# A gated attention and expert layer: which queues carry the gates' spread rows, which engine normalizes rows, and how a logarithm is corrected

## The chip, the cores and the metric

The kernel runs on one core of one Trainium2 chip, in float32. The core has five engines that run at the same time and meet through semaphores: TensorE (PE; its weight loads are listed apart as PEld), VectorE (DVE), ScalarE (ACT), GpSimd (POOL) and SyncE (SP), which only issues DMAs. Each engine takes its instructions strictly in the order that the compiled program gives it. The metric is the time of one execution on the device, in microseconds (us).

## What is computed

The reference takes x and ctx, both of shape (8, 512, 1024), so 4096 tokens of 1024 numbers. Cut to what matters:

```
n  = layernorm(x)                      # rows: (x - mean) / sqrt(var + eps)
ig = [n, ctx, ctx] @ Wi + bi           # 16 heads: input gates
fg = [n, ctx, ctx] @ Wf + bf           # forget gates
log_f = log_sigmoid(fg);  cum = cumsum of log_f along the sequence
log_D[s, t] = cum[s] - cum[t] + ig[t]  for t <= s, else -inf
D  = exp(log_D - max over t)
C  = (n_h ctx_h^T / 8) * D             # each head has 64 columns
h  = C / (max(|row sum of C|, exp(-max)) + 1e-6) @ ctx_h
x  = x + tanh(g_xattn) * layernorm of h over each head * ln_scale
y  = layernorm(x)
x  = x + tanh(g_ffn) * (shared(y) + the two best of 16 experts(y), weighted)
```

`shared` and each expert are silu(y Wg) * (y Wu) Wd.

## The kernel before, in words

**Tiles and stages.** The 4096 tokens are 32 tiles of 128 rows (four to a sequence, NT = 32, NS = 4). The first stage runs the attention over the tiles in a loop (L882 to L941) and fills TensorE's free places with units of the shared network for the first 20 tiles (`shared_units`, L225; a chunk is 16 matmuls or 16 of a projection down, and `fill` runs the next ones that the loop's shares allow). Then the tokens are gathered expert by expert (from L1301 on); that second stage is not touched by the change.

**One turn of the loop, for tile i.** It starts with the transposes of tile i+1's normalized rows (`prep_queries`, from `q.xn` to qT). `prep_weights` turns the spread gates `q.d` into weights: 16 exponents on ScalarE, each with a column of `q.cols` as bias (L603). `scores(i, 0)` multiplies qT and kT into two PSUM banks (`psc`), and VectorE multiplies the banks into d (L619). `prep_keys` transposes the context rows of tile i+1 (`q.kv` to kT). `head_norm(i - 1)` finishes the attention of the tile before on VectorE (L699 to L701). After a filler, `gate_products` and `prep_gates` make the gates of tile i+1, then `finish_rows(i - 1)` normalizes the finished rows to y, `values` multiplies weights and context (`pav`), `turn_rows(i - 1)` transposes y, `head_scale` and `grow` end the tile: `grow` adds the products `pst` to the running `state`, whose adds on VectorE (L672) free the banks that the next `psc` takes. `prep_columns(i + 1)` comes before the last filler.

**The gates (`prep_gates`, L485).** One matmul (`pg`) sums the partial products. log_sigmoid(f) is min(f, 0) - log(1 + z), with z = exp(-|f|). The logarithm is taken of the rounded u = 1 + z and corrected by the factor z / (u - 1), with a case for u = 1. Then come a running sum (`cum`), a running maximum (`m`), nm = -m, and e = exp(m of the tile before - m). The rows nm and e hold 16 heads x 128 tokens; their values are needed by all partitions. So each is written to DRAM (`nm_d`, `e_d`) and read back spread over 128 partitions: `q.d` (1 MB, one DMA) and `q.eb` (two DMAs of 256 KB, 512 pieces each). Tile 0 needs neither, and the first tile of each sequence has no e. All of these DMAs, like all loads and stores, are issued by SP, in one order.

**prep_columns (L553).** It transposes the gate rows to columns (`pc`, `cols`), masks `q.d` on GpSimd (L561), takes `decay` out of eb and multiplies eb by qT on VectorE (L567, L568), and scales the context for `grow` (`wv`).

**Normalizing a row tile.** `row_stats` (L124) takes mean and variance on VectorE. `inverse_deviation` (L115) adds eps and raises to -0.5 on GpSimd (`ve`, `rstd`). `normed` (L450) subtracts and multiplies on VectorE:

```
def normed(row, mean, rstd):
    o = wk.tile([P, D], F32, tag="row", name="row", bufs=2)
    normed.last = nc.vector.tensor_scalar(o, row, mean, rstd, ALU.subtract, ALU.mult).ins
    return o
```

It is used twice for each tile: for x two tiles ahead (`prep_norm`) and for y (`finish_rows`).

**What sets the order.** The loop is only the order of writing. A list scheduler with estimated durations places each instruction on its engine's queue; `tc.issue_after` and `pinned` hold an instruction behind a given other one. `behind` is the last matmul of the last filler unit. Buffers of a tile pool are reused in rotation (`bufs`); a load waits until the users of its buffer are done. Context rows `kv` have two buffers, x rows three.

Of the kernel before, what the change touches and what calls it, by code (L numbers as in the profile page):

```python
# [46 lines left out]
def flamingo_layer(  # L47
# [20 lines left out]
    nc = tc.nc  # L68
# [55 lines left out]
    def row_stats(pool, row):  # L124

        st = pool.tile([P, 2, 6], F32, tag="bst", name="bst")
        for k in range(2):
            nc.vector.bn_stats(st[:, k, :], row[:, k * 512 : (k + 1) * 512])
# [157 lines left out]
    def pinned(stack, ins):  # L286

        if ins:
            stack.enter_context(tc.issue_after(ins[0]))
# [20 lines left out]
    with ExitStack() as actx:  # L310
# [15 lines left out]

        def load_kv(i: int):
            q, b, c = toks[i], i // NS, i % NS
            q.kv = wk.tile([P, D], F32, tag="kv", name="kv")
            nc.sync.dma_start(q.kv, ctx_in[b, c * P : (c + 1) * P, :])  # L330

        load_x(0)
# [6 lines left out]
        nc.scalar.dma_start(w3[:, :, NH:], wf.rearrange("(c p) h -> p c h", p=P))  # L339
        bias_i = ac.tile([NH, 1], F32, name="bias_i")  # L340
        bias_f = ac.tile([NH, 1], F32, name="bias_f")
        nc.scalar.dma_start(bias_i, bi.unsqueeze(1))
        nc.scalar.dma_start(bias_f, bf.unsqueeze(1))
        ones_p = ac.tile([P, P], F32, name="ones_p")
        nc.gpsimd.memset(ones_p, 1.0)
        ones = ones_p[:NH, :]
# [33 lines left out]


        lnsc = ac.tile([P, D], F32, name="lnsc")
        nc.scalar.dma_start(lnsc, ln_scale.unsqueeze(0).to_broadcast([P, D]))


        sums = ac.tile([P, 48], F32, name="sums")
# [18 lines left out]
        nc.scalar.dma_start(acc_d[T : T + P, :], zeros[:, :D])  # L405
# [13 lines left out]
        def prep_router():  # L419
            nc.vector.tensor_scalar(lnsc, lnsc, tgx, None, ALU.mult)  # L420
            rw = wk.tile([NE, D], F32, tag="u", name="rw", bufs=1)
            nc.scalar.dma_start(rw, router_w)
# [24 lines left out]
            nc.scalar.copy(parts, pp)  # L447
            return parts

        def normed(row, mean, rstd):  # L450
            o = wk.tile([P, D], F32, tag="row", name="row", bufs=2)
            normed.last = nc.vector.tensor_scalar(o, row, mean, rstd, ALU.subtract, ALU.mult).ins
            return o

        def prep_norm(i: int):
            q = toks[i]
            mv = row_stats(sm, q.x)
            rstd = inverse_deviation(sm, mv[:, 1:2], LN_EPS, [P, 1])
            q.xn = normed(q.x, mv[:, 0:1], rstd)

        def prep_values(i: int):
            q = toks[i]
# [22 lines left out]
        def prep_gates(i: int, after=()):  # L485
            q, last, first = toks[i], i % NS == NS - 1, i % NS == 0
            pg = ps.tile([48, P], F32, tag="tr", name="pg")
            with ExitStack() as order:
                pinned(order, after)
                nc.tensor.matmul(pg, lhsT=sums, rhs=q.parts, start=True, stop=True)  # L490

            def row(name, bufs=2):
                return gt.tile([NH, P], F32, tag=name, name=name, bufs=bufs)

            f = row("f", 1)
            a, en, w = (rows3[i % 2][32 * k : 32 * k + NH, :] for k in range(3))
            nc.scalar.copy(f, pg[32:48, :])
            nc.vector.tensor_scalar(a, pg[0:NH, :], bias_i, None, ALU.add)
            nc.vector.tensor_scalar(f, f, bias_f, None, ALU.add)


            z, u, lnu, eq = (row(n, 1) for n in ("z", "u", "lnu", "eq"))
# [20 lines left out]
            nc.vector.tensor_tensor_scan(  # L523
                q.m, a, a, LOWEST if first else before.m[:, P - 1 : P], ALU.max, ALU.max
            )
            nm = row("nm", 1)
            nc.vector.tensor_scalar(nm, q.m, -1.0, None, ALU.mult)

            q.d = wk.tile([P, NH, P], F32, tag="d", name="d")
            if i > 0:  # L530
                nc.sync.dma_start(nm_d[i], nm)
                nc.sync.dma_start(q.d, nm_d[i].unsqueeze(0).to_broadcast([P, NH, P]))
            else:
                q.nm = nm
            if not first:

                e = row("e", 1)
                nc.scalar.activation(e, q.m, AF.Exp, bias=before.m[:, P - 1 : P], scale=-1.0)
                nc.sync.dma_start(e_d[i], e)
                q.eb = wk.tile([P, NC, P], F32, tag="eb", name="eb")  # L540
                for hh in range(2):
                    nc.sync.dma_start(
                        q.eb[hh * DH : (hh + 1) * DH, :, :],
                        e_d[i].rearrange("(c a) s -> a c s", a=2)[hh]
                        .unsqueeze(0).to_broadcast([DH, NC, P]),
                    )

            nc.vector.tensor_add(en, q.cum, q.m)
            nc.scalar.activation(en, en, AF.Exp, scale=-1.0)
            if not last:  # L550
                nc.scalar.activation(w, a, AF.Exp, bias=nm[:, P - 1 : P])

        def prep_columns(i: int):  # L553
            q, last, first = toks[i], i % NS == NS - 1, i % NS == 0
            pc = ps.tile([P, 5, NH], F32, tag="tr", name="pc")
            nc.tensor.transpose(pc.rearrange("p k h -> p (k h)"), rows3[i % 2], ident[:80, :80])
# [8 lines left out]
            if not first:  # L565
                q.decay = sm.tile([P, NC], F32, tag="decay", name="decay", bufs=2)
                nc.vector.tensor_copy(q.decay, q.eb[:, :, P - 1])  # L567
                nc.vector.scalar_tensor_tensor(  # L568
                    q.eb, q.eb, DH**-0.5, q.qT, ALU.mult, ALU.mult
                )  # L570
# [132 lines left out]
        def finish_rows(i: int):  # L703
            q = toks[i]
            nc.sync.dma_start(x1_d[i] if i < NT - 4 * HELD else acc_d[i * P : (i + 1) * P, :], q.x)
            mv = row_stats(sm, q.x)
            rstd = inverse_deviation(sm, mv[:, 1:2], LN_EPS, [P, 1])
            q.y = normed(q.x, mv[:, 0:1], rstd)
            nc.sync.dma_start(y_d[i * P : (i + 1) * P, :], q.y)

        def turn_rows(i: int):
# [126 lines left out]
        prep_norm(0)  # L838
        prep_queries(0)
        prep_keys(0)  # L840
        with tc.issue_after(normed.last):
# [5 lines left out]
        with tc.issue_after(normed.last):  # L847
            prep_norm(1)
        with tc.issue_after(normed.last):
            prep_router()  # L850
        prep_weights(0, 0)
        prep_weights(0, 1)
# [29 lines left out]
        for i in range(1, NT):  # L882
# [651 lines left out]
```

## Time and profile before

| what | value |
|---|---|
| median of 3 runs | 3168.99 us (3162.78 to 3174.18) |
| the profiled execution | 3176.98 us, span 3174.8 us |
| VectorE, ScalarE, GpSimd busy | 56%, 27%, 41% of the span |
| L452 row (VectorE) | 64 times, 52.3 us, mean 817 ns |
| L510 reciprocal (VectorE) | 32 times, 30.0 us, mean 936 ns |
| L561 mask on d (GpSimd) | 31 times, 63.8 us, mean 2057 ns |
| DMA d, from issue to landing | median 5.6 us |
| DMA eb, from issue to landing | median 6.9 us |
| DMA nm_d and e_d, from issue to landing | median 2.0 us each |
| DMA kv, from issue to landing | median 6.0 us |

The page shows one execution. Its first lines give the busy time of each engine; then follow the span in 40 equal slices (busy tenths, and under PEclk the granted clock of TensorE in tenths). "A <- B" behind a wait means that A stood still until B was done. A queue with a q (SPq) is the part of an engine that issues DMAs. In the timeline a row starts with its start and its length in us; what stands in brackets is the idle time ahead of it and what ended that.

### The profile page before, as it was taken

How to read it: one execution, taken by the hardware profiler on the slowest of the kernel's cores; microseconds unless marked ns; L12 is line 12 of the kernel's file. 1: busy time of each engine (PE TensorE's matmuls, PEld its weight loads, DVE VectorE, ACT ScalarE, POOL GpSimd, SP SyncE). 2: the span in 40 equal slices, each digit the busy share in tenths (PEclk: the TensorE clock that was granted, in tenths of full speed). 3: DMA queues.
4: the chain of work that ended last, by engine and by line, in shares of the span. 5: the costliest groups of instructions: out<-in, count | busy, mean ns of one | idle time of the engine just before them, and what ended most of it. 6: DMA issues, size and time to landing. Idle time of an engine off the chain costs nothing.

```text
span 3174.8 us, 42502 instructions
## 1 busy us (share of the span) xinstructions
PE 3055.4 (96%) x16193; PEld 2290.9 (72%) x16193; DVE 1792.3 (56%) x3597; ACT 859.1 (27%) x1823; POOL 1295.8 (41%) x1019
## 2 busy tenths in 40 slices
PE   6999989999999999998999999999999999999999
PEld 5778777776877768676666677777777777767776
DVE  5655656666767766653444444444544554555554
ACT  3544443544444534411111111111111111100000
POOL 2212231323232222316555555555665545444442
PEclk7989999999999999999999999999999999999999
DMA  6776565665666566545554444554555544644330
GB/s 196 207 222 184 180 168 174 178 202 164 201 177 195 181 177 188 164 131 209 136 136 119 127 134 135 134 139 134 141 141 142 149 113 133 211 161 158 113 126 27
DMA packets 371103, 500.59 MB, mean 158 GB/s; under 512 B 24304, under 2 KB 263072, under 8 KB 366768
## 3 DMA queue, kind: packets, MB, share of 16 engines
q1 hardware_dynamic: 342560, 425.00, 42.8%
q0 software_dynamic: 24576, 71.52, 10.7%
q8 instruction: 130, 2.13, 0.3%
q10 hardware_dynamic: 3760, 1.31, 0.2%
q14 instruction: 77, 0.63, 0.1%
HBM read 394.57 MB, written 113.69 MB: 160 GB/s over the span
## 4 chain that ended last, share of the span: by engine, by line
PE 50%; DVE 4%; issue 0%; DMA 0%; POOL 0%; DVEq 0%
PE pq L1330 47%; PE ptx L1248 2%; DVE hsum L1398 1%; PE pq L1437 1%; DVE hT L1352 1%; DVE hsum L1399 1%; DVE up L1351 0%; DVE tsum L1279 0%; DMA gat<-y_d,tok_i 0%; DVE tsum L1276 0%; DVE tsum L1277 0%; DVE yo L1409 0%; DVE xT L1251 0%; DVE u L1416 0%; DVE u L1415 0%
## 5 line engine op out<-in xcount | busy, mean ns | idle before, releaser
L1330 PE MATMUL pq<-xT,w 128*128 128x256 f32 (+12 forms) x2112 | 496.9, 385 | 8.6 <-DVEq L1311 8.6
L1330 PEld LDWEIGHTS pq<-xT,w 128*128 128x128 f32 x2112 | 401.3, 190 | 83.5 <-issue 11.0
L1330 PE MATMUL pq<-tsum,wsum 128*128 128x256 f32 (+12 forms) x1408 | 339.4, 384 | 0.0
L252 PE MATMUL pgu<-sh_yT,swg 128*128 128x256 f32 (+1 forms) x1280 | 299.7, 384 | 0.6 <-DMA swg<-L_ffn_shared_gate_w_dram 0.6
L1330 PEld LDWEIGHTS pq<-tsum,wsum 128*128 128x128 f32 x1408 | 264.0, 190 | 40.0
L269 PE MATMUL pso<-sh_down,sh_hT 128*128 128x512 f32 x640 | 286.6, 599 | 0.9 <-DVE sh_hT L258 0.9
L252 PE MATMUL pgu<-sh_yT,swu 128*128 128x256 f32 (+1 forms) x1280 | 276.2, 369 | 0.9 <-DMA swu<-n_L_ffn_shared_up_w_dram 0.9
L252 PEld LDWEIGHTS pgu<-sh_yT,swg 128*128 128x128 f32 x1280 | 233.7, 197 | 33.0 <-issue 3.6
L252 PEld LDWEIGHTS pgu<-sh_yT,swu 128*128 128x128 f32 x1280 | 233.7, 190 | 31.0 <-DMA swu<-n_L_ffn_shared_up_w_dram 1.3
L118 POOL TENSOR_SCALAR ve<-bmv 128x1 f32<-128x1 f32 x64 | 15.6, 243 | 576.3 <-DVE bmv L130 574.2
L1354 DVE TENSOR_TENSOR hT<-pq,u 128x256 f32<-128x256 f32 (+12 forms) x176 | 75.7, 430 | 299.1 <-PE pq L1330 294.1
L1295 POOL TENSOR_TENSOR wsum<-w 128x512 f32<-128x512 f32 x88 | 113.5, 1289 | 277.7 <-PE pq L1330 275.1
L269 PEld LDWEIGHTS pso<-sh_down,sh_hT 128*128 128x128 f32 x640 | 119.1, 192 | 135.2 <-issue 132.2
L1351 DVE TENSOR_TENSOR up<-pq,u 128x256 f32<-128x256 f32 (+12 forms) x176 | 75.6, 429 | 211.8 <-PE pq L1330 210.4
L1053 POOL DMA_INDIRECT acc_d<-yo,row_i x64 | 102.1, 1595 | 189.8 <-ACT yo L1427 81.5
L1330 PE MATMUL pq<-wd,hT 128*128 128x512 f32 x352 | 169.9, 598 | 7.1 <-DVE hT L1352 5.4
L1330 PE MATMUL pq<-tsum,w 128*128 128x256 f32 (+12 forms) x704 | 169.6, 384 | 0.0
L1330 PE MATMUL pq<-xT,wsum 128*128 128x256 f32 (+12 forms) x704 | 169.6, 384 | 0.0
L1330 PE MATMUL pq<-dsum,hsum 128*128 128x512 f32 x352 | 165.4, 592 | 0.0
L1330 PE MATMUL pq<-dsum,hT 128*128 128x512 f32 x352 | 165.4, 592 | 0.0
L1409 DVE TENSOR_TENSOR yo<-pq,u 128x512 f32<-128x512 f32 x176 | 119.1, 687 | 81.7 <-PE pq L1330 69.8
L1355 ACT ACTIVATE hT<-hT 128x256 f32<-128x256 f32 (+12 forms) x176 | 74.1, 421 | 326.5 <-DVE hT L1354 326.5
(275 smaller groups left out, 5459.1 us busy)
## 6 DMA issues: line engine op xcount, KB each, us to landing
swg<-L_ffn_shared_gate_w_dram SPq DMA_DIRECT2D x88, 512.0 KB, 4.9
swu<-n_L_ffn_shared_up_w_dram SPq DMA_DIRECT2D x88, 512.0 KB, 5.8
w<-in_L_ffn_gate_w_dram SPq DMA_DIRECT2D x16, 2048.0 KB, 10.5
w<-in_L_ffn_up_w_dram SPq DMA_DIRECT2D x16, 2048.0 KB, 10.5
wd<-in_L_ffn_down_w_dram SPq DMA_DIRECT2D x16, 2048.0 KB, 8.0
d<-nm_d SPq DMA_DIRECT2D x31, 1024.0 KB, 5.6
x_sb<-in_x_dram SPq DMA_DIRECT2D x32, 512.0 KB, 5.0
kv<-in_ctx_dram SPq DMA_DIRECT2D x32, 512.0 KB, 6.0
```

Of the source, the lines that this page charges most:

```text
L252: last = nc.tensor.matmul(pg[:, half, :n], lhsT=w[:, c, :], rhs=st["yT"][:, c, :n], start=(c == 0), stop=(c == NC - 1),)
L269: last = nc.tensor.matmul(po, lhsT=st["hT"][:, k, t * P : (t + 1) * P], rhs=sh_down[:, k, cols], start=(k == 0), stop=(k == 2 * NFC - 1),)
L1053: nc.gpsimd.indirect_dma_start(out=rows, out_offset=bass.IndirectOffsetOnAxis(ap=index, axis=0), in_=row, in_offset=None, compute_op=ALU.add,)
L1248: nc.tensor.transpose(pt[:, c, :], row[:, (half * 4 + c) * P : (half * 4 + c + 1) * P], ident)
L1295: nc.gpsimd.tensor_tensor(s1, a21, a22, ALU.add)
L1330: nc.tensor.matmul(out, lhsT=left[:, c, :], rhs=right[:, c, :], start=(c == 0), stop=(c == chunks - 1))
L1351: nc.vector.tensor_tensor(up, part, other, ALU.add)
L1352: nc.vector.tensor_tensor(out, out, up, ALU.mult)
L1354: nc.vector.tensor_tensor(out, part, other, ALU.add)
L1355: nc.scalar.activation(out, out, AF.Silu)
L1398: nc.vector.tensor_tensor(s1, a21, a22, ALU.add)
L1409: nc.vector.tensor_tensor(rows[t][:, halves[half]], part, other, ALU.add)
```

## The change

- **Queues and place of the spread rows.** nm_d and e_d are written from ScalarE's queue, d and eb are read back from GpSimd's. `decay` and the product of eb and qT move from `prep_columns` to a new `prep_state(i)`, which is called in the turn of tile i itself, behind its second scores. `prep_columns(i + 1)` moves behind the last filler unit, and its transpose is pinned there. `kv` has three buffers.
- **Rows.** `normed` is an activation on ScalarE, rstd * x + shift, with shift = -mean * rstd made on GpSimd.
- **Logarithm.** log(1 + z) is corrected by adding z - (u - 1), without a division; the bias of f is added by ScalarE in the copy out of PSUM.
- **Start.** Five loads and stores of the start (biases, ln_scale, router, zero rows) go from ScalarE's queue to GpSimd's, and three orderings of the start hang on other instructions.

```diff
-            q.kv = wk.tile([P, D], F32, tag="kv", name="kv")
+            q.kv = wk.tile([P, D], F32, tag="kv", name="kv", bufs=3)
...
-        nc.scalar.dma_start(bias_i, bi.unsqueeze(1))
-        nc.scalar.dma_start(bias_f, bf.unsqueeze(1))
+        nc.gpsimd.dma_start(bias_i, bi.unsqueeze(1))
+        nc.gpsimd.dma_start(bias_f, bf.unsqueeze(1))
...
-        def normed(row, mean, rstd):
+        def normed(row, mv):
+
+            rstd = inverse_deviation(sm, mv[:, 1:2], LN_EPS, [P, 1])
+            shift = sm.tile([P, 1], F32, tag="shift", name="shift")
+            nc.gpsimd.tensor_scalar(shift, mv[:, 0:1], rstd, -1.0, ALU.mult, ALU.mult)
             o = wk.tile([P, D], F32, tag="row", name="row", bufs=2)
-            normed.last = nc.vector.tensor_scalar(o, row, mean, rstd, ALU.subtract, ALU.mult).ins
+            normed.last = nc.scalar.activation(o, row, AF.Identity, scale=rstd, bias=shift).ins
             return o
...
-            nc.scalar.copy(f, pg[32:48, :])
+            nc.scalar.activation(f, pg[32:48, :], AF.Identity, bias=bias_f)
             nc.vector.tensor_scalar(a, pg[0:NH, :], bias_i, None, ALU.add)
-            nc.vector.tensor_scalar(f, f, bias_f, None, ALU.add)
...
             nc.vector.tensor_scalar(u, z, 1.0, None, ALU.add)
             nc.scalar.activation(lnu, u, AF.Ln)
-            nc.vector.tensor_scalar(u, u, -1.0, None, ALU.add)
-            nc.vector.tensor_scalar(eq, u, 0.0, None, ALU.is_equal)
-            nc.vector.tensor_add(u, u, eq)
-            nc.vector.reciprocal(u, u)
-            nc.vector.tensor_mul(u, u, z)
-            nc.vector.tensor_mul(lnu, lnu, u)
-            nc.vector.tensor_mul(eq, eq, z)
-            nc.vector.tensor_add(lnu, lnu, eq)
-            nc.vector.scalar_tensor_tensor(f, f, 0.0, lnu, ALU.min, ALU.subtract)
+            nc.vector.scalar_tensor_tensor(u, u, -1.0, z, ALU.add, ALU.subtract)
+            nc.vector.scalar_tensor_tensor(f, f, 0.0, u, ALU.min, ALU.add)
+            nc.vector.tensor_sub(f, f, lnu)
...
-                nc.sync.dma_start(nm_d[i], nm)
-                nc.sync.dma_start(q.d, nm_d[i].unsqueeze(0).to_broadcast([P, NH, P]))
+                nc.scalar.dma_start(nm_d[i], nm)
+                nc.gpsimd.dma_start(q.d, nm_d[i].unsqueeze(0).to_broadcast([P, NH, P]))
...
-                nc.sync.dma_start(e_d[i], e)
+                nc.scalar.dma_start(e_d[i], e)
                 q.eb = wk.tile([P, NC, P], F32, tag="eb", name="eb")
                 for hh in range(2):
-                    nc.sync.dma_start(
+                    nc.gpsimd.dma_start(
...
-        def prep_columns(i: int):
-            q, last, first = toks[i], i % NS == NS - 1, i % NS == 0
+        def prep_state(i: int):
+
+            q = toks[i]
+            if i % NS == 0:
+                return
+            q.decay = sm.tile([P, NC], F32, tag="decay", name="decay", bufs=2)
+            nc.vector.tensor_copy(q.decay, q.eb[:, :, P - 1])
+            nc.vector.scalar_tensor_tensor(q.eb, q.eb, DH**-0.5, q.qT, ALU.mult, ALU.mult)
+
+        def prep_columns(i: int, after=()):
+            q, last = toks[i], i % NS == NS - 1
             pc = ps.tile([P, 5, NH], F32, tag="tr", name="pc")
-            nc.tensor.transpose(pc.rearrange("p k h -> p (k h)"), rows3[i % 2], ident[:80, :80])
+            with ExitStack() as order:
+                pinned(order, after)
+                nc.tensor.transpose(pc.rearrange("p k h -> p (k h)"), rows3[i % 2], ident[:80, :80])
...
             scored = scores(i, 1)
+            prep_state(i)
             if nxt:
                 prep_gates(i + 1, scored)
...
+            fill(share)
             if nxt:
-                prep_columns(i + 1)
-            fill(share)
+                prep_columns(i + 1, behind)
```

More of the change, by code (lines that the diff above doesn't have):

```diff
@@ L127, in row_stats @@
         for k in range(2):
-            nc.vector.bn_stats(st[:, k, :], row[:, k * 512 : (k + 1) * 512])
+            row_stats.last = nc.vector.bn_stats(st[:, k, :], row[:, k * 512 : (k + 1) * 512]).ins
         mv = pool.tile([P, 2], F32, tag="bmv", name="bmv")
@@ L382, in flamingo_layer @@
         lnsc = ac.tile([P, D], F32, name="lnsc")
-        nc.scalar.dma_start(lnsc, ln_scale.unsqueeze(0).to_broadcast([P, D]))
+        nc.gpsimd.dma_start(lnsc, ln_scale.unsqueeze(0).to_broadcast([P, D]))
         sums = ac.tile([P, 48], F32, name="sums")
@@ L404, in flamingo_layer @@
         zeros = state.rearrange("p c e -> p (c e)")
-        nc.scalar.dma_start(acc_d[T : T + P, :], zeros[:, :D])
+        nc.gpsimd.dma_start(acc_d[T : T + P, :], zeros[:, :D])
         zero80 = ac.tile([P, NT_], F32, name="zero80")
@@ L421, in prep_router @@
             rw = wk.tile([NE, D], F32, tag="u", name="rw", bufs=1)
-            nc.scalar.dma_start(rw, router_w)
+            nc.gpsimd.dma_start(rw, router_w)
             nc.vector.memset(rwT, 0.0)
@@ L456, in prep_norm @@
             q = toks[i]
-            mv = row_stats(sm, q.x)
-            rstd = inverse_deviation(sm, mv[:, 1:2], LN_EPS, [P, 1])
-            q.xn = normed(q.x, mv[:, 0:1], rstd)
+            q.xn = normed(q.x, row_stats(sm, q.x))
         def prep_values(i: int):
@@ L496, in prep_gates @@
             a, en, w = (rows3[i % 2][32 * k : 32 * k + NH, :] for k in range(3))
-            nc.scalar.copy(f, pg[32:48, :])
+            nc.scalar.activation(f, pg[32:48, :], AF.Identity, bias=bias_f)
             nc.vector.tensor_scalar(a, pg[0:NH, :], bias_i, None, ALU.add)
-            nc.vector.tensor_scalar(f, f, bias_f, None, ALU.add)
-            z, u, lnu, eq = (row(n, 1) for n in ("z", "u", "lnu", "eq"))
+            z, u, lnu = (row(n, 1) for n in ("z", "u", "lnu"))
             nc.vector.scalar_tensor_tensor(z, f, -1.0, f, ALU.mult, ALU.min)
@@ L526, in prep_gates @@
             nm = row("nm", 1)
-            nc.vector.tensor_scalar(nm, q.m, -1.0, None, ALU.mult)
+            q.gated = nc.vector.tensor_scalar(nm, q.m, -1.0, None, ALU.mult).ins
             q.d = wk.tile([P, NH, P], F32, tag="d", name="d")
             if i > 0:
-                nc.sync.dma_start(nm_d[i], nm)
-                nc.sync.dma_start(q.d, nm_d[i].unsqueeze(0).to_broadcast([P, NH, P]))
+                nc.scalar.dma_start(nm_d[i], nm)
+                nc.gpsimd.dma_start(q.d, nm_d[i].unsqueeze(0).to_broadcast([P, NH, P]))
             else:
@@ L564, in prep_columns @@
                 ).ins
[L565 to L570, printed above, removed]
             if not last:
@@ L705, in finish_rows @@
             nc.sync.dma_start(x1_d[i] if i < NT - 4 * HELD else acc_d[i * P : (i + 1) * P, :], q.x)
-            mv = row_stats(sm, q.x)
-            rstd = inverse_deviation(sm, mv[:, 1:2], LN_EPS, [P, 1])
-            q.y = normed(q.x, mv[:, 0:1], rstd)
+            q.y = normed(q.x, row_stats(sm, q.x))
             nc.sync.dma_start(y_d[i * P : (i + 1) * P, :], q.y)
@@ L840, in flamingo_layer @@
         prep_keys(0)
-        with tc.issue_after(normed.last):
+        with tc.issue_after(row_stats.last):
             prep_gate_weights()
@@ L846, in flamingo_layer @@
         prep_columns(0)
-        with tc.issue_after(normed.last):
+        with tc.issue_after(toks[0].gated):
             prep_norm(1)
-        with tc.issue_after(normed.last):
             prep_router()
```

## The prediction

> **What bounds the kernel now.** I read the page first, then a table of stages, then the waits by engine, then the timeline of one tile.
>
> ```profile
> PE 3055.4 (96%) x16193; PEld 2290.9 (72%) x16193; DVE 1792.3 (56%) x3597; ACT 859.1 (27%) x1823; POOL 1295.8 (41%) x1019
> PE   6999989999999999998999999999999999999999
> PEclk7989999999999999999999999999999999999999
> ```
>
> TensorE (PE) is busy for 96% of the span. Its work is fixed and the change leaves it alone, so all that can be won is idle PE time and time at a lower granted clock. The diff touches only the attention stage: the first matmul of the expert stage starts at 1454.67 us in the timeline. In the table of 40 us windows, a bad and a good window of that stage read:
>
> ```profile
> 200.00:240.00 40.00, 35.21 (x222) 25.66 (x221) 25.33 (x64) 16.48 (x39) 10.43 (x8) 0.74 0.47 158
> 1000.00:1040.00 40.00, 40.00 (x247) 26.16 (x245) 29.55 (x59) 15.53 (x39) 9.55 (x8) 1.00 0.62 185
> ```
>
> The columns are window, length, then busy time of PE, PEld, DVE, ACT, POOL, then clock, DMA share, GB/s. Between 80 and 1440 us the PE gaps in the timeline add up to 62 us, and the windows' missing clock, the sum of (1 - clock) x 40, is 48 us, some 40 us of which fell on busy PE. The first 80 us hold 31 us more of gaps. So the whole prize is about 62 + 40 us plus part of the start: 3% at most. Each microsecond of gap comes with 40/62 = 0.65 us of lost clock, so I price gaps at 1.65. What ends the gaps (waits of PE up to 1460 us; us, times, longest):
>
> ```profile
> PE pt L434 <- DVE row L452: 29.2, 9, 9.9
> PE pt L434 <- DMA kv<-in_ctx_dram: 15.1, 8, 3.5
> PE pm L590 <- DVE nm L527: 9.2, 1, 9.2
> ...
> PE pl L733 <- ACT parts L447: 5.1, 3, 3.2
> PE pc L556 <- ACT rows L549: 5.1, 2, 4.6
> PE psc L612 <- DVE state L672: 4.7, 3, 2.1
> ```
>
> Of the 29.2 us for normalized rows, 18.3 are two gaps of the start (9.9 and 8.36). The other 11 us, and 5 us that the list books to `cols` and `slot` in front of the same transposes, are VectorE (DVE) coming late to y. The 15.1 us are kv loads that came late. Behind PE stand these waits of the other engines and of SP's queue (all engines, and SP from 80 to 1440 us):
>
> ```profile
> POOL d L561 <- DMA d<-nm_d: 137.1, 18, 15.5
> DVE decay L567 <- DMA eb<-e_d: 55.1, 14, 8.1
> SPq L531 <- DVE rows L548: 94.3, 28, 10.3
> SPq L532 <- DMA nm_d<-nm: 34.0, 20, 5.8
> SPq L330 <- PE pst L663: 34.1, 11, 6.4
> ```
>
> SP stands still for nm (94.3) and for its landing (34.0), and every load behind it stands too; a kv load also waits for the tile two back to release its buffer. One tile shows it all:
>
> ```profile
> 402.30 0.46 DVE L523 TENSOR_TENSOR_SCAN m<-rows,m 16x128 f32<-16x128 f32 x1
> 405.76 1.26 SPq L542 DMA_DIRECT2D eb<-e_d  x2
> 409.60 1.15 PE L663 MATMUL pst<-wv,kv 128*64 128x65 f32 x32
> 417.36 1.16 PE L612 MATMUL psc<-qT,kT 64*128 64x128 f32 x16
> 419.20 0.17 DVE L567 COPY decay<-eb 128x8 f32<-128x8 f32 x1 [5.24 <-DMA eb<-e_d]
> 422.03 1.06 PE L434 MATMUL pt<-ident,kv 128*128 128x128 f32 x8 [3.50 <-DMA kv<-in_ctx_dram]
> 425.84 1.28 DVE L619 SCALAR_TENSOR_TENSOR d<-psc,d 128x512 f32<-128x512 f32 x2
> 433.69 0.81 DVE L452 TENSOR_SCALAR row<-x_sb,bmv,rstd 128x1024 f32<-128x1024 f32 x1 [0.77 <-POOL rstd L121]
> ```
>
> DVE loses 5.24 us to eb and 0.99 to kv before it reaches the scores (d), and the row follows the scores at a fixed distance.
>
> **The change, part by part.** Durations are the means of before.
>
> *kv in three buffers, spread rows off SP.* Removed from SP: 31 nm_d (0.33 us), 31 d (0.34), 24 e_d (about 0.5), 48 eb (0.62), some 63 us of issuing. Here the Trainium skill speaks against the change: "DMA: Bandwidth & Descriptors", section "Issuing engines are not separate DMA queues", says that all issuers' transfers interleave on the same engines, and issuing from several saves only the sequencer's time. By the rule this part wins nothing, as SP's issuing is not PE's limit. The rows say that SP's in-order waiting (94.3 + 34.0) is what is lost, and that 15.1 us of it reach PE. I take the rows: -14 us of gaps. Bounds: 0 (transfers late for bandwidth) and -15.1.
>
> *Rows by ScalarE (ACT).* DVE loses 64 x 0.817 = 52.3 us. No ACT row has this width: 128x128 takes 278 ns and 128x256 384, so 0.83 ns a column, and a pointer operand adds 386 - 278 = 108 ns; 1024 columns with two pointers come to 1.24 us, 79 us for 64. The skill's "ScalarE: Activation LUTs", "Rules for kernel authors", would leave multiply and add on VectorE. Taken alone that is right: the chain of one row becomes 0.42 us longer, plus 0.24 us for `shift` on POOL (row L118: 243 ns), so by the rule +0.7 us on each of 31 y rows that PE waits for, up to +21 us. But DVE has 26 of 40 us filled and ACT 17, and the row's place is set by what precedes it: without the wait for eb (5.24), decay and scaling (1.4) and late kv (1), DVE is held in the tile above only by ACT's exponents (start 419.42, first eight done at about 422), so d starts some 3 us earlier. Net 2.5 us earlier; the gaps are 0.5 to 3 us. I take -12 of the 16 us; bounds -16 and +5. ACT also issues 55 DMAs (0.33 to 0.5 us) but has ten table loads fewer in its compiled order (10 x 1.28): about even.
>
> *Logarithm.* Nine DVE steps after Ln (96.0 us in 32 tiles) and the bias step (8.5) go, three of 0.274 us come: with the rows, DVE's work falls by 130 us. In series the steps from Ln to nm shrink by 2.7 us, so m, nm and e come 2.7 us earlier in each tile.
>
> *prep_columns behind the last filler unit.* The gap for `rows` (5.1 us) is covered by a unit of 3.6 to 7 us: -5. Behind it wait only `cols` (0.2 us), and it stands ahead of the qT copies and the table load (2.4 us), which cover it. Cover gone: +0.4 us a tile.
>
> *POOL.* Added: 64 shifts (15.6 us) and 79 DMA issues. The nearest row is its indirect DMA of 128 rows, 1.0 us; eb has 512 pieces a transfer, so I bound it by 1.0 and 2.5 us. 95 to 167 us on an engine with 10 of 40 us filled. Its `d` issue waits for nm_d to land (2.0 us); behind it stand eb, the mask on d, hrstd and the next rstd. POOL already waits 137.1 us for d, so that is no new kind of wait.
>
> *eb "half a tile later".* In the source decay and scaling move behind the second scores. In DVE's compiled order they don't: they stand at the end of the tile before, in 13 of the 24 tiles with only 2 to 3.3 us of DVE work between m and decay (mean 5.0; before 6.8 by the same count), ahead of v, var and the four state adds. eb lands at m + 0.4 (e) + 0.4 (issue) + 2.0 (e_d) + 3 x 1.0 (POOL) + about 5 (issue to landing: 4.6 for POOL's small gathers, 6.9 for eb on SP) = about m + 11 us. So DVE waits longer than 55.1 us in all; it has the time, but not everywhere. In the tile above, state adds must be done when psc starts, 15 us after m, 17.5 with m earlier; they come at 11 + 1.4 (decay, eb) + 4.5 (sh_base, v, var) + 1.7 = 18.6. That is 1 us late in each of 13 tiles: +13 us of gaps. Bounds: 0 (eb at m + 10) and 4.5 us a tile (POOL at 2.5 us for each eb).
>
> *Start.* ACT's bias_i issue alone lasted 6.49 us (2.23 to 8.72), and PE waited 2.44 us for ACT. That goes; POOL's issues and the shift delay the first row by about 2.5 us; nm comes 3 to 5 us earlier. Net -4.
>
> **Sum.** Gaps -14 -12 -5 +13 = -18, times 1.65 = -30, start -4: -34 us. Against the profiled execution, 3176.98 us (span 3174.8), that is 3143; the median of the runs, 3168.99, lies 8 lower, so 3135.
>
> **Rivals.**
> *eb late (slower).* DVE stands at decay, and psc waits for the banks that the state adds release. Each microsecond late in the 13 tiles costs 13 x 1.65 = 21 us; without it the gain is 31 x 1.65 + 4 = 55, so it decides from 2.6 us, that is eb later than m + 12.6. At 4.5 us it gives +42: 3211. For: the compiled order, and gaps for state gave the two longest stretches at half clock (behind 148 and 231 us). It would also come true if VectorE holds POOL off SBUF while POOL writes descriptors, which the skill (same DMA page, "SWDGE vs HWDGE vs iDMA") warns of; no row here shows it. Against: m comes earlier, and in 11 tiles the distance is 6.4 us or more.
> *ACT becomes the wait (no change).* The row stands in ACT's queue behind its waits (57.1 us for z, 49.0 for e); the 12 us are not won and the ACT gaps (yT and parts, 9 us) double: -34 + 21 x 1.65 = +1, 3170.
> *All of it.* With DVE 130 us lighter, state and yT gaps go as well, and 12 us are left: -50 x 1.65 - 6 = -88, 3081.
>
> **Numbers.** Forecast 0.60 (3100 to 3158), all of it 0.08, no change 0.10, eb late 0.22. The measurement can tell 0.3% from no change, 9.5 us. Faster 0.69, same 0.10, slower 0.21. The range, 3085 to 3192, leaves out the lower part of "all of it" and the upper half of "eb late", some 18%.
>
> **What would show it.** Right: PE's waits for kv under 3 us and for L563 none; PE's waits for the row, now from ACT, under 5 us behind 80 us; DVE's wait for eb 100 us or more, with PE's waits for state under 20. Wrong: PE's waits for state at 40 us or more with half clock behind them (eb late), or pt waiting for ACT in most tiles (ACT), or POOL's eb issues far from 1 us.

## The result and the profile after

The changed kernel takes 3272.52 us (median of 4 runs, 3254.22 to 3281.48) against 3171.59 us of the kernel before on the same chip (3162.78 to 3177.67): ratio 1.0298, 95% interval 1.0269 to 1.0327. It is 3% slower, where the prediction was 1.1% faster and its range ended at 3192.

The profiled execution took 3254.22 us, its span 3252.4. It is the fastest of the four, and the one before (3176.98) is among the slower of its own, so the traces show 77.6 us of the 101 by which the medians differ. The first matmul of the expert stage starts at 1531.31 us instead of 1454.67, 76.6 us later, and the spans differ by 77.6: all of the loss that the traces show lies in the attention stage. From the page, busy time and the two rows of tenths:

```profile
PE 3074.1 (95%) x16193; PEld 2300.8 (71%) x16193; DVE 1646.8 (51%) x3309; ACT 924.8 (28%) x1877; POOL 1376.0 (42%) x1167
PE   5888999989899989998999999999999999999999
PEclk8998999999999999999999999999999999999999
```

VectorE has 145.5 us less work than before, as the change meant, and TensorE is idle for longer. The same two windows as before (other work falls into them now):

```profile
200.00:240.00 40.00, 34.49 (x279) 24.33 (x279) 22.25 (x55) 22.91 (x51) 9.57 (x10) 0.99 0.60 196
1000.00:1040.00 40.00, 34.01 (x228) 29.20 (x228) 19.83 (x51) 20.64 (x43) 21.22 (x22) 0.91 0.67 176
```

The first has about as much idle TensorE as before (5.5 us against 4.8) at nearly the full clock; the second, good before, has 6 us of it and a tenth of the clock is gone. Over the windows from 80 to 1400 us, idle TensorE went from 62.1 to 117.3 us (+55.2), and the clock not granted, the sum of (1 - clock) x 40, from 48.0 to 68.4 us (+20.4). Together 75.6 us, close to the 76.6 us of the stage. (The second sum counts idle time too; on busy TensorE alone it rose by 16.0 us, and the two make 71.2.) What ends the gaps (waits of PE up to 1480 us; total, times, longest):

```profile
PE pl L732 <- ACT parts L447: 41.6, 13, 8.9
PE pt L434 <- DVE cols L565: 34.8, 10, 10.4
PE pt L434 <- ACT row L456: 26.6, 10, 11.8
PE psc L613 <- DVE state L671: 14.7, 3, 8.2
PE psc L613 <- DVE state L673: 13.1, 6, 5.7
```

Kv (15.1 us before) is gone from this list, and so is the 5.1 us that `pc` waited for the gate rows. In their place stand `parts` on ScalarE (5.1 us before) and `cols` on VectorE (3.4 before). The waits of the other engines say what is behind them:

```profile
ACT row L456 <- POOL shift L454: 196.9, 50, 15.5
DVE decay L555 <- DMA eb<-e_d: 129.3, 17, 17.8
POOL d L568 <- DMA d<-nm_d: 114.2, 24, 9.2
POOL d L528 <- DMA nm_d<-nm: 52.7, 9, 12.1
POOL d L528 <- DMA e_d<-e: 39.8, 5, 19.5
```

The last two are new: GpSimd stands still before it can issue d, until rows that were written to DRAM have landed. With eb's issues (16.0 for e_d and 15.0 for nm_d) that is 123.5 us. The writes themselves, now on ScalarE's queue, also land later: the last number is the median time to landing, and it was 2.0 us from SP before.

```profile
nm_d<-nm ACTq DMA_DIRECT2D x31, 8.0 KB, 3.3
```

One place of the timeline shows how a late issue travels. m of this tile ended at 826.6, and nm_d and e_d were issued by 827.7:

```profile
831.63 0.97 POOL L812 DMA_INDIRECT table_d<-rowid,slots_i  x1 [0.30 <-issue]
832.59 0.62 POOL L528 DMA_DIRECT2D d<-nm_d  x1
833.20 1.46 POOL L538 DMA_DIRECT2D eb<-e_d  x2
841.20 2.02 POOL L568 TENSOR_SCALAR_AFFINE_SELECT d<-d 128x2048 f32<-128x2048 f32 x1 [6.55 <-DMA d<-nm_d]
843.31 0.24 POOL L118 TENSOR_SCALAR ve<-bmv 128x1 f32<-128x1 f32 x1
844.15 0.17 DVE L555 COPY decay<-eb 128x8 f32<-128x8 f32 x1 [13.80 <-DMA eb<-e_d]
845.67 1.24 ACT L456 ACTIVATE row<-x_sb,shift,rstd 128x1024 f32<-128x1024 f32 x1 [15.52 <-POOL shift L454]
848.50 0.26 ACT L447 COPY parts<-pp 128x128 f32<-128x128 f32 x1
848.81 0.61 PE L732 MATMUL pl<-sums,parts 128*128 128x16 f32 x2 [8.88 <-ACT parts L447]
```

The spread rows are issued 6.0 to 8.1 us after m. In this place it is GpSimd's own table scatters (the row DMA_INDIRECT and others like it) that they stand behind, and not a landing. The mask on d waits for d, and `ve` of the next row, whose statistics were ready at 829.25, stands behind the mask. ScalarE waits 15.52 us for shift; this is a row of x, which nobody needs yet (its transposes come at 859.7), but `parts` stands behind it in ScalarE's order, and TensorE waits 8.88 us for `parts`. VectorE stands 13.80 us at decay at the same time.

### The profile page after: what moved, and what is told of

Same layout as the page of the kernel before. It is cut to its first block, busy times and chain, and to the rows that moved or that the text cites. A ratio compares the mean times of both kernels' runs of the same rounds, so it can differ in the third digit from the quotient of the medians.

```text
span 3252.4 us, 42336 instructions
## 1 busy us (share of the span) xinstructions
PE 3074.1 (95%) x16193; PEld 2300.8 (71%) x16193; DVE 1646.8 (51%) x3309; ACT 924.8 (28%) x1877; POOL 1376.0 (42%) x1167
## 4 chain that ended last, share of the span: by engine, by line
PE 48%; DVE 4%; issue 0%; DVEq 0%
PE pq L1329 46%; PE ptx L1247 1%; DVE hsum L1397 1%; PE pq L1436 1%; DVE hT L1351 1%; DVE hsum L1398 1%; DVE up L1350 0%; DVE tsum L1278 0%; DVE tsum L1275 0%; DVE tsum L1276 0%; DVE yo L1408 0%; DVE xT L1250 0%; DVE u L1415 0%; DVE hT L1399 0%; DVE u L1414 0%
## 6 DMA issues: line engine op xcount, KB each, us to landing
w<-in_L_ffn_gate_w_dram SPq DMA_DIRECT2D x16, 2048.0 KB, 10.4
```

## The experiments

Ratios are to the kernel before, run beside each version, with the 95% interval. "Hold" pins decay and the scaling of eb on VectorE behind the tile's first scores.

| run | kernel | us | ratio |
|---|---|---|---|
| e1 | after, spread rows on SP | 3204.79 | 1.0083 (1.0049 to 1.0118) |
| e2 | after, rows on VectorE | 3256.21 | 1.0247 (1.0203 to 1.0291) |
| e3 | after, columns ahead of the filler | 3223.35 | 1.0139 (1.0097 to 1.0180) |
| e4 | before, short logarithm | 3184.95 | 1.0028 (1.0013 to 1.0043) |
| e5 | after, hold | 3283.58 | 1.0343 (1.0314 to 1.0372) |
| e6 | after, spread rows on SP, hold | 3201.27 | 1.0080 (1.0053 to 1.0107) |
| e7 | before, hold | 3188.61 | 1.0042 (1.0028 to 1.0056) |
| e8 | before, short logarithm, hold | 3172.16 | 0.9983 (0.9970 to 0.9997) |
| e9 | e1 and e3 together | 3200.83 | 1.0065 (1.0040 to 1.0090) |
| e10 | e1 and e2 together | 3211.93 | 1.0098 (1.0073 to 1.0123) |
| e11 | after, only e_d and eb on SP | 3242.93 | 1.0183 (1.0152 to 1.0214) |
| e12 | after, only nm_d and d on SP | 3245.77 | 1.0210 (1.0187 to 1.0233) |
| e13 | after, x rows held on ScalarE | 3256.43 | 1.0255 (1.0236 to 1.0274) |
| e14 | before, spread rows on POOL and ACT | 3230.39 | 1.0167 (1.0149 to 1.0184) |
| e15 | before, short logarithm, kv in three buffers, hold | 3161.95 | 0.9945 (0.9928 to 0.9961) |
| e16 | after, all spread rows on ACT | 3240.60 | 1.0211 (1.0182 to 1.0240) |
| e17 | e1, e2 and e3 together | 3174.28 | 1.0016 (0.9998 to 1.0035) |
| e18 | e17, hold | 3170.34 | 0.9994 (0.9976 to 1.0012) |

**One part undone, one part done (e1 to e4).** The first theory: GpSimd's queue makes eb and the rows late, and VectorE, standing at decay, passes it on.

```diff
# e1 (nm_d, e_d and eb likewise)
-                nc.gpsimd.dma_start(q.d, nm_d[i].unsqueeze(0).to_broadcast([P, NH, P]))
+                nc.sync.dma_start(q.d, nm_d[i].unsqueeze(0).to_broadcast([P, NH, P]))
# e2
-            normed.last = nc.scalar.activation(o, row, AF.Identity, scale=rstd, bias=shift).ins
+            normed.last = nc.vector.tensor_scalar(o, row, mv[:, 0:1], rstd, ALU.subtract, ALU.mult).ins
# e3
+            if nxt:
+                prep_columns(i + 1)
             fill(share)
-            if nxt:
-                prep_columns(i + 1, behind)
```

e4 is the diff's part on the logarithm, laid on the kernel before.

> The changed kernel with one part undone: all spread-row transfers (nm_d, d, e_d, eb) issued by SP's queue again; kv keeps three buffers, rows stay on ACT, short logarithm, columns behind the filler. Theory 'POOL's queue' (d and eb are issued late by POOL, in order behind its table scatters and waiting for nm_d and e_d to land; DVE then stands at decay for eb, and the row's rstd and shift stand on POOL behind the mask on d): this gives nearly all of the 101 us back, time 3150 to 3190; DVE's wait for eb falls from 129 us to under 60, ACT's wait for shift from 197 to under 100, PE's pl wait for parts from 41.6 to under 15. Rival 'rows on ACT' (the row blocks ACT's queue ahead of parts, sh_act and u): stays at 3230 or more, pl's wait for parts stays above 25 us. Rival 'columns' (pc right before the next transposes exposes the copy of cols on DVE): stays at 3230 or more, pt's wait for cols above 25 us.

> The changed kernel with one part undone: the rows are normalized by VectorE again (no shift on POOL). Theory 'POOL's queue': the row's wait for rstd only moves from ACT to DVE, eb stays late: 3240 or more, DVE's wait for eb still above 100 us; PE's pl wait for parts falls under 15 us, but waits for row, state and cols grow in its place. Rival 'rows on ACT': 3190 or less, since the 41.6 us of pl and the 14.9 us of row behind 80 us go, times about 1.3. Rival 'columns': about 3270, with cols at 35 us.

> The changed kernel with one part undone: the columns of the next tile are prepared ahead of the filler again and their transpose is not pinned behind it. Theory 'POOL's queue': cols is late only because DVE stands at decay for eb, so the wait reappears at other DVE results: 3245 or more, PE's wait for cols under 15 us but state and row larger. Rival 'columns': 3272 minus 34.8 x 1.3, about 3225, with DVE's wait for eb unchanged. Rival 'rows on ACT': about 3270, pl's wait for parts still 40 us.

> The kernel before with one part done: the short logarithm and the forget bias in ACT's copy, nothing else. My prediction took 96.0 + 8.5 us of DVE steps away against three of 0.274 us a tile, m 2.7 us earlier in each tile, and booked no gap to it directly. Theory 'm earlier is worth something' (the nm gap of the start, 9.2 us, shrinks by 2.7, and d, eb land 2.7 us earlier): 20 to 45 us faster, 3125 to 3150, DVE's wait for eb under 40 us. Rival 'DVE has slack, nothing moves' (an earlier m only makes SP and POOL wait earlier): 3160 to 3172. Rival 'planner moves eb earlier in DVE's order': slower, up to 3200, DVE's wait for eb above 80 us.

e1 gave 2.15 of the 2.98%, some 68 us: the largest single part, but less than expected. PE's waits in e1:

```profile
PE pt L434 <- DVE cols L565: 36.4, 14, 7.1
PE pt L434 <- ACT row L456: 21.9, 9, 12.3
PE psc L613 <- DVE state L671: 14.6, 3, 8.1
PE pl L732 <- ACT parts L447: 11.8, 6, 4.1
```

`parts` fell from 41.6 to 11.8, and ACT's wait for shift from 196.9 to 118.6 us, its longest from 15.5 to 5.9; `cols` stayed. But VectorE's wait for eb stayed too, at 133.1 us where under 60 was expected: this wait does not come from GpSimd's queue. e3 gave 49 us, as the columns' rival said (3225 expected, 3223 measured, VectorE's wait for eb unchanged at 127.0). e2 gave 16, as the first theory said: `parts` fell to 7.2 us and `cols` rose to 52.8. The parts are not additive: alone they give 68, 49 and 16 us, and the loss is 101. And the logarithm alone made the kernel slower by 0.28%, with eb's wait up from 55.1 to 114.4 us: of the three expectations only the third has its sign. VectorE does less and comes to decay sooner; that this is what made it slower is not shown.

**Is the wait at decay the cost? (e5 to e8).** The same two instructions, really held back:

```diff
-            nc.vector.tensor_copy(q.decay, q.eb[:, :, P - 1])
-            nc.vector.scalar_tensor_tensor(q.eb, q.eb, DH**-0.5, q.qT, ALU.mult, ALU.mult)
+            with tc.issue_after(q.first_scored):
+                nc.vector.tensor_copy(q.decay, q.eb[:, :, P - 1])
+                nc.vector.scalar_tensor_tensor(q.eb, q.eb, DH**-0.5, q.qT, ALU.mult, ALU.mult)
...
+            if g == 0:
+                q.first_scored = q.scored
```

In e7 and e8, `prep_state` also moves behind the second scores as in the change.

> The changed kernel with decay and the scaling of eb really held back: pinned on VectorE behind the multiplication of the tile's first scores, so that VectorE doesn't reach them at the end of the tile before. Spread rows still come from POOL and ACT. Theory 'DVE stands at decay': the 129 us wait for eb falls under 15 us, PE's waits for cols (34.8) and state (27.8) fall under 20 together, time 3272 - 60 = about 3210 (3190 to 3225); what stays is pl's wait for parts (41.6), which comes from POOL. Rival 'POOL's queue': eb lands as late as before and the row waits as long for the mask on d; pl's wait stays near 40 us and the time at 3240 or more. Rival 'pav takes the wait': scaling eb behind the scores makes pav late by 1.4 us in each tile, PE waits 20 us or more for eb, no gain.

> The changed kernel with both undone: spread rows issued by SP, and decay and scaling pinned on VectorE behind the first scores' multiplication. Theory 'DVE stands at decay, and POOL holds the rows': both losses go, 3205 of the run with SP alone less its 133 us wait for eb, which fed 36.4 us of cols and 20 us of state waits: about 3205 - 55 = 3150 (3130 to 3170), under the kernel before. Rival 'rows on ACT and the columns' order cost what is left': 3185 or more, with PE's waits for row and parts above 30 us and for cols above 25.

> The kernel before with one thing changed: decay and the scaling of eb pinned on VectorE behind the multiplication of the tile's first scores, nothing else. Theory 'DVE stands at decay': before lost 55.1 us of VectorE's time to eb, with some 10 to 20 us of PE gaps behind it (row L452 29.2 of which 11 behind the start, state 8.5), so 10 to 30 us faster: 3148 to 3168, eb's wait under 10 us. Rival 'VectorE has the time': within 0.3%, 3170 to 3188, as POOL's mask or SP's order becomes late next.

> The kernel before with the short logarithm and with decay and scaling pinned behind the first scores' multiplication. The log alone took 9 us more than before, with eb's wait up from 55 to 114 us and gaps up from 62 to 74. Theory 'the shorter logarithm only brings VectorE to decay sooner': with decay held, this wait is gone and what the log saves shows: 5 to 25 us under the kernel before with decay held alone, about 3140. Rival 'the shorter chain has no taker': the same time as the kernel before with decay held, within 8 us.

Not by this test. In e5 no wait for eb is left in the list of VectorE's waits, and the kernel is not faster (1.0343 against 1.0298). PE's waits in e5:

```profile
PE pt L434 <- ACT row L456: 50.9, 13, 11.7
PE pl L735 <- ACT parts L447: 37.1, 10, 8.3
PE pt L434 <- DVE cols L566: 24.3, 9, 8.0
PE psc L614 <- DVE state L676: 14.1, 4, 6.7
PE psc L614 <- DVE state L674: 12.7, 3, 7.3
```

`cols` fell by 10 us, the row took 24 more, and state stayed (26.8 against 27.8 us). e6 shows the same with SP (3201 against 3205). Taking 129 us of waiting from VectorE gained nothing, and the theory fell. The hold has effects of its own, though. e8 is 0.45% under e4, and e7 is 0.42% above the kernel before: on the kernel before, the hold gains with the short logarithm and loses without it. In the changed kernel it gains nothing, with GpSimd's queue or with SP's (e5, e6).

**Which part of the spread rows, and how the parts add (e9 to e12).** These combine edits shown above; e11 and e12 send only the named two tensors by SP.

> The changed kernel with two parts undone: spread rows issued by SP, and columns prepared ahead of the filler. Rows stay on ACT, short logarithm, kv in three buffers. The theory that held decay to be the cause has fallen (eb's wait went, the time stayed). New theory, 'two parts, two costs': POOL's queue makes the row late (from bmv to the finished row 5.00 us with POOL, 3.27 with SP, 2.33 before), and the transpose of the columns right in front of the next tile's transposes makes PE wait for cols (36.4 us with SP). Both undone: 3205 less 36 x 1.2 = about 3160 (3150 to 3175), cols wait under 15 us. Rival 'one cost seen twice' (undoing the columns gave 49 us only because it brought the row forward): 3190 to 3205, with PE's row wait grown to 40 us or more.

> The changed kernel with two parts undone: spread rows issued by SP, and rows normalized by VectorE. Columns stay behind the filler. Theory 'two parts, two costs': the row is no longer late, but PE still waits some 35 us or more for cols: 3185 to 3205, PE's wait for the row about 29 us as before. Rival 'rows on ACT cost what is left with SP': 3165 or less, since from bmv to the finished row it is 2.3 us again.

> The changed kernel with e_d and eb issued by SP; nm_d stays on ACT and d on POOL. Theory 'POOL's queue, by its length': of three transfers of a tile two leave POOL (1.4 us of issuing, the waits for e_d to land, 39.8 + 16.0 us), d still waits for nm_d (52.7): about half of the 68 us that SP gave, 3225 to 3250. Rival 'the mask behind d alone holds the row': the d issue stays late by nm_d, 3255 or more. Rival 'eb alone is the cost': 3205 or less.

> The changed kernel with nm_d and d issued by SP; e_d stays on ACT and eb on POOL. Theory 'POOL's queue, by its length': 0.65 us of issuing and the wait for nm_d (52.7 us) leave POOL, the wait for e_d stays: 3225 to 3250. Rival 'the mask behind d alone holds the row': d lands earlier by some 2 us, the mask and the row come earlier, 3215 or less. Rival 'eb alone is the cost': 3255 or more.

e11 and e12 each give about half of what e1 gives (1.15 and 0.88% of 2.15%). So both d and eb cost on that queue. How long GpSimd stands does not measure the cost: it stood 68.5 us for nm_d in e11 and 111.3 for e_d in e12, against 123.5 for both in the changed kernel. And each of these runs moves the writes from ScalarE's queue to SP together with the reads; no run has only the reads on GpSimd, so how much of the cost belongs to the later landing of nm_d and e_d is not known. In e1 nm_d lands as fast as before:

```profile
nm_d<-nm SPq DMA_DIRECT2D x31, 8.0 KB, 1.7
```

In e9 and e10 one more part undone beside e1 gives nothing: cols falls to 11.1 us in e9, and PE's wait for the row grows from 21.9 to 37.5; in e10 the row is quick again but cols stays at 37.7. "Two parts, two costs" fell: in e9 the row's wait grew as the rival said, to a little under its 40 us.

The timeline gives, for each row, the time from its statistics (bmv) to its end: 2.33 us on average before, 5.00 after (20 of 64 rows over 5 us), 3.27 in e1, 3.62 in e2, 2.47 in e10. So rows on ScalarE cost 0.8 us of it with SP, as predicted (+0.7), and 1.4 with GpSimd's queue.

**How GpSimd's late work gets to TensorE (e13 to e16).** e13 pins the ACT row of x, two tiles ahead, behind the tile's last square; e16 is e1 with `nc.scalar` for all four. Of e13's edit only the call is shown; `prep_norm` and `normed` hand the list on to the ACT row.

```diff
# e13
-                prep_norm(i + 2)
+                prep_norm(i + 2, [toks[i].squared])
```

> The changed kernel with one thing held back: the ACT row of the tile after next (the x row of prep_norm) is pinned behind the tile's last square, so that it no longer stands ahead of parts, u and sq in ACT's order. All else, POOL's queue too, as changed. Theory 'POOL's queue makes the row late, and ACT's queue passes it on': the row waits up to 15.5 us for shift and parts stands behind it, so PE's pl wait for parts falls from 41.6 us to under 12; the time falls by 25 to 50 us, 3222 to 3247, with the wait for cols left or grown. Rival 'eb and d late are the cost, parts only shows it': 3255 or more. Rival 'rows on ACT in this place are all of it': 3205 or less.

> The kernel before with one part done: d and eb issued by POOL, nm_d and e_d by ACT; kv stays in two buffers, rows on VectorE, long logarithm, columns ahead of the filler. Theory 'POOL's queue costs by itself': with rows on VectorE the changed kernel lost 44 us to it (3256 against 3212), so here 30 to 55 us over before: 3210 to 3235, PE's waits for kv under 5 us, waits for row and cols above 60. Rival 'it costs only through ACT's rows and the moved state': within 10 us of before, 3170 to 3190.

> The kernel before with the short logarithm, kv in three buffers, and decay and scaling pinned behind the first scores' multiplication; spread rows on SP, rows on VectorE, columns ahead of the filler. With two kv buffers this was 3172, 0.17% under before, with 3.6 us of PE waits for kv left. Theory 'kv in three buffers takes the last of the kv wait': 3165, 0 to 10 us less. Rival 're-planning moves more than these parts are worth': anywhere from 3160 to 3195, with PE's gaps for row, cols and state other than in the run with two buffers.

> The changed kernel with d and eb issued by ACT instead of POOL; nm_d and e_d stay on ACT, so no spread row is on SP or POOL. Theory 'the queue that is made to wait for nm_d and e_d decides': POOL is free (rows' shift early, bmv to row under 4 us), but ACT now stands for nm_d and e_d to land (about 2.5 us each, twice a tile) ahead of en, w, u and the row: 3215 to 3260. Rival 'only POOL is the wrong queue': 3205 or less, as with SP. Rival 'any queue but SP delays the issue alike': 3265 or more.

e13: `parts` is gone as a wait (2.1 us), as the theory said, and the time falls by only some 14 us by the ratios, with intervals that touch. That is the rival's time (3255 or more: `parts` only shows the lateness). Another wait took its place:

```profile
PE pt L434 <- DVE cols L567: 63.4, 14, 9.3
PE pl L734 <- ACT parts L447: 2.1, 2, 1.3
```

The ACT rows are one outlet of GpSimd's lateness and not its source. e14 shows the queues alone: with rows on VectorE, the long logarithm and the old place of decay and columns, the spread rows' queues cost 1.67%, 53 us. GpSimd's waits in e14:

```profile
POOL d L561 <- DMA d<-nm_d: 87.3, 19, 9.1
POOL d L532 <- DMA nm_d<-nm: 66.4, 13, 13.4
POOL d L532 <- DMA e_d<-e: 16.7, 2, 8.5
```

The rows' chain is as quick as before (2.31 us) and VectorE's wait for eb no longer (49.6 us). Yet the mask ends 14.0 us after m instead of 12.2, ScalarE's exponents wait 15.0 us for it (1.3 before), VectorE's state adds 14.9 us for GpSimd's product (6.4 before). Idle TensorE (80 to 1400 us) rises by 25.9 us and the clock not granted by 29.6, together 55.5; the expert stage starts 54.2 us later. PE's wait for kv rose to 25.3 us with two buffers, although SP had less to issue, where under 5 was expected; some 10 of the 25.9 us are this wait, which three buffers take away, so the 53 us are not all a cost of the changed kernel. The waits for row and cols were expected above 60 us and came to 34.7 for the row and none for cols.

e16: on ScalarE the rows cost less than on GpSimd (2.11 against 2.98%) and more than on SP (0.83%). ACT and POOL compute for TensorE, and SP does not, which fits. But the row's chain is 4.75 us long with GpSimd free of these issues, and under 4 was expected. e15 is the fastest version, 0.55% under the kernel before; its waits for kv are gone.

**What is left with SP (e17, e18).**

> The changed kernel with three parts undone: spread rows on SP, rows on VectorE, columns ahead of the filler. What stays of the change: short logarithm, kv in three buffers, decay and scaling moved in the source (not held back), the start's small loads on POOL. Theory 'decay not held back costs what is left': with the short logarithm, holding it was worth 13 us (3185 against 3172), so 3175 to 3190 with eb's wait on VectorE above 90 us. Rival 'the start's loads on POOL cost it': the first tiles late by 5 us or more, m of the second tile no earlier than in the kernel before. Rival 'rows on ACT cost it': 3160 to 3168, like the version that is best so far.

> As the run with spread rows, rows and columns undone, and decay and scaling pinned behind the first scores' multiplication. It differs from the best version so far (3162) by the start's loads on POOL alone. Theory 'decay not held back costs what is left': 3158 to 3170, 10 to 20 us under its neighbour of this call. Rival 'the start costs it': 3172 or more, late from the first tiles on. Rival 're-planning': no ordered difference between the two.

With rows and columns both undone beside the spread rows, the kernel is back at the time of before (1.0016), though each of them alone gave nothing (e9, e10). So some 0.7% (0.83 less 0.16) belong to these two together. Holding decay gives 0.22% more, inside the two intervals. e18 differs from e15 by the start's loads alone, and is 0.49% slower; m of the second tile comes 6.4 us later than in e15. That need not be the cause: of the two profiled executions e18's is the faster (3165.57 against 3169.40), and it reaches the expert stage 4.5 us earlier. What the start's loads cost is not settled.

## Why the prediction was wrong

**The step that failed** is GpSimd's: "POOL already waits 137.1 us for d, so that is no new kind of wait." The issue itself I had put at 1.0 to 2.5 us; it took 0.65 (d) and 0.72 (eb), 31 x 0.65 + 48 x 0.72 = 55 us in all. But it is issued in order, and 123.5 us of standing for nm_d and e_d came with it, on an engine that makes rstd, shift, hrstd, the state's product and the mask. Such a wait is a new kind: before, it was SP that stood for nm_d. I listed what is queued behind ("eb, the mask on d, hrstd and the next rstd") and booked nothing for it. Alone the move of the spread rows costs 53 us (e14), 10 us of idle for kv included; undone in the changed kernel it gives back 68 (e1).

**The gain of the queues, -14.** The kv gaps went, but they are gone in e1 too, where SP issues the spread rows, and they grew in e14, where it does not: three buffers did it. The rule of the Trainium skill that I weighed and set aside ("DMA: Bandwidth & Descriptors", "Issuing engines are not separate DMA queues": another issuer saves only the sequencer's time) was right here: to take issuing from SP won nothing. Landing of d and eb took the same from SP in e1 (7.4 us for d, 7.9 for eb) as from GpSimd in the changed kernel (6.8 and 7.7). The waits that I read on SP (94.3 + 34.0) are waits of work that must come first; they moved to GpSimd, where they cost. (The issue times that I called means are medians; by means SP's issuing was 67 us and not 63.)

**Rows, -12.** The row took 1.245 us as estimated (1.24). But PE's wait for it behind 80 us was 12.3 us and not under 5, and the row in ScalarE's order made `parts` wait. The rival "ACT becomes the wait" had the place (parts), and took for it only doubled ACT gaps (9 to 18 us); they became 43, nearly five times as long, as the shift from GpSimd came late. Undone alone, it is worth 16 us (e2), with SP nothing (e10).

**Columns, -5, "Cover gone: +0.4 us a tile".** The wait of `pc` went. `pc` and the transposes take turns in one PSUM pool of two buffers, so the next transposes, right behind it, waited for the copy of `cols` in VectorE's queue, up to 10.4 us:

```profile
1195.30 0.23 PE L563 MATMUL pc<-ident,rows 80*128 80x80 f32 x1
1196.87 1.00 DVE L555 COPY decay<-eb 128x8 f32<-128x8 f32 x1 [17.82 <-DMA eb<-e_d]
1206.10 0.21 DVE L565 COPY cols<-pc 128x48 f32<-128x48 f32 x1
1206.36 1.12 PE L434 MATMUL pt<-ident,row 128*128 128x128 f32 x4 [10.39 <-DVE cols L565]
```

Here it was VectorE's wait for eb that held the copy back; without that wait, in e5, `cols` still cost 24.3 us. The price of the copy (0.2 us) was not the price of its place. Undone alone: 49 us (e3).

**eb late, +13, and the rival at 3211.** eb came later than I said: m + 17.5 us in the place shown, and m + 14.2 on average over the 14 tiles whose landing the trace has, where I had m + 11 and 12.6 as the point of decision. The estimate was too early from the start: in the kernel before, by the same count, eb landed at m + 12.6, and with SP in e1 at m + 14.1. VectorE's wait of 129.3 us is as predicted (100 or more), PE's waits for state came to 27.8, between my two marks (20 and 40). But e5 takes the wait for eb away, and neither the time nor the waits for state (26.8) fall. The rival had the sign and not the cause.

**Start, -4.** m of the second tile did come earlier, at 67.05 us instead of 73.55, but idle TensorE in the first 80 us rose from 31.7 to 35.9. The gain did not show.

**Logarithm.** VectorE's work fell by 145.5 us (predicted 130). I gave it no gap directly, and took from it only that m comes earlier; alone it is 0.28% slower (e4).

**The factor 1.65** for lost clock: counted on busy TensorE as I did, (55.2 + 16.0) / 55.2 = 1.3 in the changed kernel, and (25.9 + 26.1) / 25.9 = 2.0 in e14. A fixed factor is too coarse for a single case.

Not settled: how much of the cost is GpSimd's queue and how much the later landing of the writes from ScalarE's; by which of GpSimd's late results it reaches `cols` and TensorE; why e14 lost more by the clock than by idle time; and how far the effects under 0.5% (e4, e7, e8) are the parts' own, since each edit also re-plans all engines' orders.

## What to carry to other kernels

A DMA that must wait for another to land should be issued by a queue on which nothing else is urgent: the wait moves with it, and all work behind it in order pays. Before work is put on an engine that is 40% busy, list what is queued behind each of its waits and who needs that next; busy shares say nothing on it. And a long wait on a profile need not be the cost: take it away alone, and see whether the time moves.

## What the hardware showed that was not expected

GpSimd's issue of a transfer with 512 pieces took 0.72 us, hardly more than SP's 0.62, but that of d took 0.65 against 0.34 (medians). Writes of 8 KB landed 3.3 us after their issue on ScalarE's queue in the changed kernel, and 1.7 us on SP's in e1. Gaps of similar sum cost different clock: from 80 to 1400 us, e14 had 88.0 us idle and 77.6 us of clock not granted, e1 79.0 and 48.4.
